# Two more key tiles per slot in three fp32r products, the pointwise residual on ScalarE and VectorE, and joined small operations, in a fused attention and convolution kernel

## The chip, the cores and the metric

The kernel runs on one core of one Trainium2 chip. The core has TensorE (matmuls; its weight loads are listed apart), VectorE (DVE in the profile), ScalarE (ACT), GpSimd (POOL) and SyncE (SP), each of which takes its own instructions in order, and 16 DMA engines. The metric is the device time of one execution in microseconds. A profile is one further execution with the hardware profiler on; its span runs from the first to the last instruction.

## The reference

The input is x of 4 pictures x 64 x 64 pixels x 256 channels, in float32. Layer 0 is full self-attention over the 4096 pixels of each picture:

```
q, k, v = x@Wq + bq, x@Wk + bk, x@Wv + bv        # 32, 32 and 256 wide
x = gamma * softmax(q k^T) v + x
```

Layer 1 takes that result h:

```
perceived = depthwise 3x3 convolution, 3 outputs per channel  # 768 channels
dx        = w_up2 @ gelu(w_up1 @ perceived + b_up1) + b_up2   # 768 -> 512 -> 256, per pixel
h_new     = h + dx                                            # the pointwise residual
h_attn    = softmax-weighted sum of the 9 neighbours' values  # 3x3 local attention, q, k, v from h_new
out       = h_new + h_attn
```

Neighbours outside the picture have score 0 and value 0, so they count in the local softmax's denominator alone. The program first computes without subtracting a maximum from the scores, watches for overflow in a few sums, and has a second, slower path that runs if any was seen.

## The kernel before, in words

**Slots.** A block is 8 picture rows, 512 pixels; there are 8 blocks per picture and 32 in all (`NSLOT`). Slot s runs the full attention of block s, and beside it layer 1 of earlier blocks: the 3x3 convolution of block s - 2, the hidden layer, pointwise residual, local scores and local values of block k = s - 3, and the local attention's result of block a = s - 5. The order of all instructions is written out by hand in the main loop (lines 1214 to 1359), which the engines' queues keep. A slot has 16 points. At each point the loop issues loads, ScalarE's high parts and TensorE's energy for later halves, one entry of `jobs` (layer 1), the product of this point's half, VectorE's sums and parts for the next half (`add_up`), and some steps of the convolution on VectorE. The list `share` (L1244) says how many of the 54 convolution steps (42 taps on 526 pixels, 12 combinations of half-size tiles) are issued at each point.

**Halves and tiles.** The 4096 keys of a picture are 16 halves n = 0 to 15 of 256 keys, and a half is two tiles (i = 0, 1) of 128 keys. For each half, TensorE makes scores for two tiles x 512 queries (`energy`, L414), ScalarE takes exp of them (L423), and `product` (L452) multiplies the weights p with the values v into the accumulators, two channel halves per tile. The product of half n stands at point n, its exp two halves earlier.

**Products in parts.** An f32 matmul appears in the profile as two records, an fp32r matmul as one. Where a tile is taken in parts, p is split into high (ScalarE), low and gap (two VectorE operations), and the f32 product of each channel half is replaced by three fp32r products with stored forms of v: high with v's high, low and gap with two further forms. The even halves 2 to 14 have both tiles in parts at once (`in_parts`, `high_part`, tiles ph, pl, pg; forms vf loaded from packed_f). The odd halves are treated tile by tile (`alone`, L228, `load_alone`, `high_alone`, `low_and_gap` at L440): the second tile of every odd half (tiles vo, oh, ol, og, four buffers under the tag vs), and also the first tile for those in `BOTH_IN_PARTS`, whose form, high, low and gap lie in the four quarters of a hidden-layer tile (tag hid, one buffer), free after the residual at point 7. This holds in full slots: slots 3 to 30 other than those whose number is 7 modulo 8, so 25 slots. `alone(s, n)` gives the tiles of half n that are taken alone. `load_alone` and `high_alone` for half n stand at point n - 1, `low_and_gap` in `add_up` at point n - 1, before that point's convolution steps. The forms were written by `project_v` (L342) one picture ahead.

**Sums.** For most halves the weights are summed by accumulating DMAs that GpSimd issues (`send`). VectorE sums halves 14 and 15 in the tile den, and in the first slot of a picture also halves 0 and 1. After half 15 `partial_sums` (L539) transposes and reduces the sums, and at point 0 of the next slot `finish` scales the accumulated result.

**The residual and after.** `update(s, c)` at points 6 and 7 multiplies the hidden layer with w_up2 for channel half c and adds bias and h, per column half, on VectorE (L863). `border_terms` (L988) then makes, with c = 1, weighted sums over the channels of the block's border pixels in the tile edge (ScalarE for one channel half, VectorE for the other); `border` at point 14 sums them over partitions by a matmul with a column of ones (L1004). `local_values` (L1016; points 0 and 10) projects 2 x 128 pixels and adds the bias in two VectorE operations. PSUM tiles for these jobs come from a rotation of two banks (`job_bank`).

Of the kernel before, what the change touches and what calls it, by code (L numbers as in the profile page):

```python
# [9 lines left out]
F32 = mybir.dt.float32  # L10
# [6 lines left out]
P = 128  # L17
# [33 lines left out]
BELOW = 1.0 - 2.0**-13  # L51
IN_PARTS = (2, 4, 6, 8, 10, 12, 14)
ONE_IN_PARTS = (1, 3, 5, 7, 9, 11, 13, 15)
BOTH_IN_PARTS = (11, 13)
BY_DMA = (3, 5, 7, 9, 11, 13)
BY_DMA_IF_FULL = tuple(range(14))

# [5 lines left out]
def attention_then_perception_kernel(  # L63
# [37 lines left out]
    def unshifted():  # L101
# [120 lines left out]
        def full(s):  # L222
            return in_two_sums(s) and s > 1 and s % NBLK < NBLK - 1
# [3 lines left out]

        def alone(s, n):  # L228

            return [i for i, ns in enumerate((BOTH_IN_PARTS, ONE_IN_PARTS)) if full(s) and n in ns]  # L230

        def load_parts(to, s, which):
            pair, r = divmod(s, 2)
# [74 lines left out]
        def load_values(s, G):  # L308
            values[s, G] = tile_of([P, TPB, C], "v", f"v_{s}_{G}", 2)
            to = values[s, G].rearrange("p t c -> p (t c)")  # L310
            at = block(s, G)
            if not in_two_sums(s):
                nc.sync.dma_start(out=to, in_=packed_v[:, bass.ts(at, TPB * C)])
            elif full(s):
                nc.sync.dma_start(out=to, in_=packed_h[:, at])
            else:
                nc.sync.dma_start(out=to[:, : 2 * C], in_=packed_h[:, at, : 2 * C])
                nc.sync.dma_start(out=to[:, 2 * C :], in_=packed_v[:, bass.ts(2 * at + 1, 2 * C)])
# [8 lines left out]
        def load_alone(s, n):  # L327
            for i in alone(s, n):
                if i:
                    f, *rest = [tile_of([P, NB], "vs", f"vo_{s}_{n}", 4)] + [None] * 3  # L330
                else:
                    four = tile_of([P, NHC, NB], "hid", f"vo_{s}_{n}_0")
                    f, *rest = (four[:, j] for j in range(NHC))
                forms[s, n, i], rests[s, n, i] = f, rest
# [96 lines left out]
        def high_alone(s, n):  # L431
            for i in alone(s, n):
                high = rests[s, n, i][0]
                if high is None:
                    high = tile_of([P, NB], "vs", f"oh_{s}_{n}", 4)
                p = weights[s, n // 2, n % 2][:, i, :]
                nc.scalar.activation(high.bitcast(F32R), p, AF.Identity, scale=BELOW)  # L437
                highs[s, n, i] = high

        def low_and_gap(s, n):  # L440
            for i in alone(s, n):
                high, (_, low, gap) = highs[s, n, i], rests.pop((s, n, i))
# [3 lines left out]
                nc.vector.tensor_tensor(low.bitcast(F32R), p, high, ALU.subtract)  # L446
                nc.vector.scalar_tensor_tensor(
                    gap.bitcast(F32R), low, -SPLIT, high, ALU.mult, ALU.add
                )
                lows[s, n, i], gaps[s, n, i] = low, gap  # L450

        def product(s, G, half):  # L452
            p = weights[s, G, half]
            n = 2 * G + half
            if n == 0:
                accs[s] = [bank("acc", f"acc_{s}_{c}") for c in range(2 * CH if in_two_sums(s) else CH)]
                started[s] = set()
            v = values[s, G][:, 2 * half : 2 * half + 2]
            todo = []
            if in_parts(s, G, half):  # L460
                f = forms.pop((s, G, half))
                for w, to, x in (
                    (v, 0, highs[s, G, half]), (f[:, :2], 0, lows[s, G, half]),
                    (f[:, 2:], CH, gaps[s, G, half]),
                ):
                    todo += [(w[:, i], to, x[:, i, :], F32R) for i in range(2)]
            else:
                apart = alone(s, n)
                todo += [(v[:, i], 0, p[:, i, :], F32) for i in range(2) if i not in apart]
                for i in apart:  # L470
                    at = s, n, i
                    f = forms.pop(at)
                    todo += [
                        (v[:, i], 0, highs[at], F32R), (f[:, :C], 0, lows[at], F32R),
                        (f[:, C:], CH, gaps[at], F32R),
                    ]
            ends = {0: n == 2 * NG - 1, CH: n == (2 * NG - 1 if full(s) else IN_PARTS[-1])}
            for k, (w, to, x, kind) in enumerate(todo):
                last = ends[to] and all(later[1] != to for later in todo[k + 1 :])
                for c in range(CH):  # L480
                    nc.tensor.matmul(  # L481
                        accs[s][to + c], lhsT=w[:, bass.ts(c, P)].bitcast(kind), rhs=x.bitcast(kind),
                        start=to not in started[s], stop=last,
                    )
                started[s].add(to)
# [53 lines left out]
        def partial_sums(s):  # L539


            a = shared(s)
            parts_[s] = tile_of([P, 2, NJ], "parts", f"parts_{s}")
            turneds[s] = tile_of([P, CH, NB], "xc", f"turned_{s}", 2)
            todo = [sums[s][:, 0, :]] + ([] if a is None else [lsums.pop(a)])
            for i, t in enumerate(todo):
                nc.vector.transpose(turneds[s][:, i, :], t)
                nc.vector.tensor_reduce(
                    parts_[s][:, i, :], squares(turneds[s][:, i, :]), axis=AX.X, op=ALU.add
                )  # L550
            watch(parts_[s][:, : len(todo), :].rearrange("p i j -> p (i j)"))

        def on_all(values, turned, out, copy=nc.vector.tensor_copy):

# [297 lines left out]
        def update(s, c):  # L852
            if c == 0:
                below(s)
            ps = job_bank(f"dx_{s}_{c}")
            for d in range(NHC):
                nc.tensor.matmul(  # L857
                    ps, lhsT=wup2[:, d, bass.ts(c, P)], rhs=hids[s][:, d, :],
                    start=(d == 0), stop=(d == NHC - 1),
                )  # L860
            for half in range(2):
                cols = slice(half * KW, (half + 1) * KW)
                nc.vector.scalar_tensor_tensor(  # L863
                    hs[s][:, c, half, HALO:, :],
                    ps.rearrange("p (h w) -> p h w", w=W)[:, :, cols],
                    bup2[:, c : c + 1],
                    xv[:, c, ring(s) : ring(s) + RB, 1 + cols.start : 1 + cols.stop],
                    ALU.add, ALU.add,
                )
            if c == CH - 1:  # L870
                border_terms(s)

# [93 lines left out]
        def edge_row(s):  # L966
            return {0: 0, NBLK - 1: RB - 1}.get(s % NBLK)

        edge = pool.tile([P, 2 * RB + W], F32, tag="edge", name="edge")

        def border_parts(s):

# [15 lines left out]
        def border_terms(s):  # L988


            for to, of in border_parts(s):
                nc.scalar.mul(edge[:, to], of(0), wc[:, 0:1])
                nc.vector.scalar_tensor_tensor(
                    edge[:, to], of(1), wc[:, 1:2], edge[:, to], ALU.mult, ALU.add
                )

        def border(s):

# [2 lines left out]
            row = edge_row(s)  # L1001
            n_side = 2 * RB
            n = border_parts(s)[-1][0].stop
            nc.tensor.matmul(ps[0:1, :n], lhsT=ones[:, 0:1], rhs=edge[:, :n], start=True, stop=True)  # L1004
# [11 lines left out]
        def local_values(s, t):  # L1016
            ps = job_bank(f"lv_{s}_{t}")
            for half in range(2):
                for kin in range(CH):
# [2 lines left out]
                        lhsT=keys_of(s, t, half, kin), rhs=wlv[:, kin, :],  # L1022
                        start=(kin == 0), stop=(kin == CH - 1),
                    )
            for half in range(2):
                if s < NSLOT - 2:
                    lvs[s, t, half] = tile_of([P, C], "lv", f"lv_{s}_{t}_{half}", 8)
                else:
                    if not half:
                        late[s, t] = late_tile(f"lv_{s}_{t}")  # L1030
                    lvs[s, t, half] = late[s, t][:, half * C : (half + 1) * C]
                lv = lvs[s, t, half]
                nc.vector.tensor_tensor(lv, ps[:, half * C : (half + 1) * C], blv, ALU.add)
                if s >= NSLOT - 1:

                    square = tile_of([P, 2, NB], "den", f"lv_{s}_{t}_{half}_2")[:, 0, :C]
                    nc.gpsimd.tensor_tensor(square, lv, lv, ALU.mult)
                    watch(square)

        def pieces(s):  # L1040

# [172 lines left out]
        for slot in range(NSLOT):  # L1214
# [611 lines left out]
```

## Time and profile before

| | |
|---|---|
| median of 3 runs | 3206.65 us (3204.02 to 3208.27) |
| profiled execution: time, span | 3203.15 us, 3201.4 us |
| granted TensorE clock | 0.998 |
| busy: TensorE, VectorE, ScalarE, GpSimd | 3179.4, 2903.6, 1550.8, 759.6 us |
| exp on ScalarE (L423) | 512 of 128x1024, 1025 ns each |
| convolution tap on VectorE (L687) | 1260 of 128x526, 759 ns each |
| low and gap of a single tile (ol, og) | 200 each, 709 and 732 ns |
| residual on VectorE (L863) | 128 of 128x256, 475 ns each |
| load of a single tile's forms (vo) | 250 of 256 KB, 3.9 us to landing |
| DMA queues | 683.26 MB, mean 213 GB/s |

In the profile a line such as "L447 DVE ... og<-ol,oh" is one group of instructions: source line, engine, tile written and tiles read. In a timeline the first two numbers are the start and the length in microseconds from the span's start. Consecutive instructions of a pipeline overlap by some 0.08 us on VectorE and more on TensorE, so the distance from start to start is what an instruction costs; in the chain of work that ended last, each piece has just that length. "x2" at the end merges two equal ones. A stretch sum gives the busy time of each engine between two times.

### The profile page before, as it was taken

How to read it: one execution, taken by the hardware profiler on the slowest of the kernel's cores; microseconds unless marked ns; L12 is line 12 of the kernel's file. 1: busy time of each engine (PE TensorE's matmuls, PEld its weight loads, DVE VectorE, ACT ScalarE, POOL GpSimd, SP SyncE). 2: the span in 40 equal slices, each digit the busy share in tenths (PEclk: the TensorE clock that was granted, in tenths of full speed). 3: DMA queues.
4: the chain of work that ended last, by engine and by line, in shares of the span. 5: the costliest groups of instructions: out<-in, count | busy, mean ns of one | idle time of the engine just before them, and what ended most of it. 6: DMA issues, size and time to landing. Idle time of an engine off the chain costs nothing.

```text
span 3201.4 us, 39239 instructions
## 1 busy us (share of the span) xinstructions
PE 3179.4 (99%) x12486; PEld 2261.7 (71%) x12486; DVE 2903.6 (91%) x4428; ACT 1550.8 (48%) x2068; POOL 759.6 (24%) x1055
## 2 busy tenths in 40 slices
PE   9999999999999999999999999999999999999998
PEld 5557777766777777776777777777677777777655
DVE  5778999998999999998999999998899999999894
ACT  4435555445545555544555545554555555455331
POOL 3201122212222221222122232211221222222121
PEclk9999999999999999999999999999999999999999
DMA  7768888777888888877878888886788888888100
GB/s 259 229 170 218 227 226 224 220 230 229 227 227 243 243 218 229 221 208 247 234 219 232 225 240 234 238 221 197 269 238 221 224 228 227 235 237 220 50 25 28
DMA packets 315588, 683.26 MB, mean 213 GB/s; under 512 B 100384, under 2 KB 101424, under 8 KB 315248
## 3 DMA queue, kind: packets, MB, share of 16 engines
q1 hardware_dynamic: 243008, 435.69, 42.6%
q0 software_dynamic: 64688, 231.54, 31.7%
q10 hardware_dynamic: 7680, 13.44, 1.1%
q8 instruction: 104, 1.70, 0.2%
q14 instruction: 108, 0.88, 0.1%
HBM read 412.46 MB, written 80.61 MB: 154 GB/s over the span
## 4 chain that ended last, share of the span: by engine, by line
PE 94%; DVE 3%; DMA 1%; issue 0%; POOL 0%; ACT 0%; SPq 0%; ACTq 0%; DVEq 0%; POOLq 0%
PE acc L481 46%; PE e L418 7%; PE dx L857 7%; PE hid_de L800 5%; PE hid_gf L800 5%; PE hid_bc L800 5%; PE lv L1020 3%; PE g L953 3%; PE lo L1154 3%; PE v L347 3%; PE s L1061 2%; PE hid_a L800 2%; DVE perc L687 1%; PE qk L272 1%; PE hid L832 1%; DMA vo<-packed_o 0%
## 5 line engine op out<-in xcount | busy, mean ns | idle before, releaser
L687 DVE SCALAR_TENSOR_TENSOR perc<-xp,wb,perc 128x526 f32<-128x526 f32 (+1 forms) x1356 | 937.7, 757 | 0.4
L423 ACT ACTIVATE p<-e 128x1024 f32<-128x1024 f32 x512 | 524.9, 1025 | 485.9 <-PE e L418 409.4
L481 PE MATMUL acc<-p,v 128*128 128x512 f32 x1472 | 678.9, 596 | 0.2 <-ACT v L363 0.2
L500 POOL DMA_DIRECT2D sent<-p x304 | 258.0, 855 | 1353.6 <-ACT p L423 823.0
L481 PEld LDWEIGHTS acc<-p,v 128*128 128x128 f32 x1472 | 275.1, 190 | 267.9 <-issue 257.6
L418 PE MATMUL e<-qa,ka 128*128 128x512 f32 x1024 | 357.1, 430 | 5.3 <-ACT p L423 1.5
L428 ACT ACTIVATE ph<-p 128x1024 fp32r<-128x1024 f32 x203 | 215.1, 1060 | 198.4 <-PE acc L481 134.7
L510 DVE TENSOR_TENSOR pl<-p,ph 128x1024 fp32r<-128x1024 f32 x203 | 256.1, 1262 | 16.8 <-ACT ph L428 16.8
L481 PE MATMUL acc<-ph,v 128*128 128x512 f32 x812 | 264.3, 447 | 0.2
L520 DVE SCALAR_TENSOR_TENSOR pg<-pl,ph 128x1024 fp32r<-128x1024 f32 x203 | 253.3, 1248 | 11.9 <-DVE pl L510 0.5
L418 PEld LDWEIGHTS e<-qa,ka 128*128 128x128 f32 x1024 | 190.9, 188 | 86.0 <-issue 39.9
L437 ACT ACTIVATE oh<-p 128x512 fp32r<-128x512 f32 x200 | 126.4, 632 | 248.4 <-PE acc L481 83.2
L857 PE MATMUL dx<-hid,wup 128*128 128x512 f32 x512 | 229.8, 592 | 0.0
L481 PE MATMUL acc<-pl,vf 128*128 128x512 f32 x812 | 223.3, 397 | 0.0
L481 PE MATMUL acc<-pg,vf 128*128 128x512 f32 x812 | 219.1, 391 | 2.0 <-DVE pg L520 2.0
L481 PEld LDWEIGHTS acc<-ph,v 128*128 128x128 f32 x812 | 148.2, 189 | 51.9 <-issue 26.8
L481 PE MATMUL acc<-oh,v 128*128 128x512 f32 x400 | 184.8, 543 | 0.0
L481 PEld LDWEIGHTS acc<-pg,vf 128*128 128x128 f32 x812 | 152.3, 188 | 39.1 <-DVE pg L520 3.3
L481 PEld LDWEIGHTS acc<-pl,vf 128*128 128x128 f32 x812 | 152.7, 188 | 37.1
L823 ACT ACTIVATE hid<-hid,bup 128x512 f32<-128x512 f32 x120 | 80.3, 716 | 199.1 <-DVE hid L807 199.1
L693 DVE TENSOR_TENSOR perc<-perc 128x262 f32<-128x262 f32 x360 | 170.8, 488 | 6.3
L857 PEld LDWEIGHTS dx<-hid,wup 128*128 128x128 f32 x512 | 96.7, 189 | 98.5 <-issue 93.4
(231 smaller groups left out, 5476.1 us busy)
## 6 DMA issues: line engine op xcount, KB each, us to landing
sent<-p POOLq DMA_DIRECT2D x356, 512.0 KB, 6.5
vf<-packed_f SPq DMA_DIRECT2D x203, 512.0 KB, 5.7
v<-packed_h SPq DMA_DIRECT2D x200, 512.0 KB, 4.7
ka<-packed SPq DMA_DIRECT2D x1016, 64.0 KB, 3.3
vo<-packed_o SPq DMA_DIRECT2D x250, 256.0 KB, 3.9
xp<-in_x SPq DMA_DIRECT2D x30, 528.0 KB, 6.9
packed_f<-vlg POOLq DMA_DIRECT2D x28, 512.0 KB, 4.3
xc<-in_x SPq DMA_DIRECT2D x56, 256.0 KB, 4.3
```

Source lines behind the costliest of these rows:

```text
L418: nc.tensor.matmul(e[:, i, :], lhsT=keys[s, G][:, bass.ts(2 * half + i, P)].bitcast(F32R), rhs=queries[s].bitcast(F32R), start=True, stop= ...
L423: nc.scalar.activation(p, e, AF.Exp)
L428: nc.scalar.activation(high.bitcast(F32R), weights[s, G, half], AF.Identity, scale=BELOW)
L437: nc.scalar.activation(high.bitcast(F32R), p, AF.Identity, scale=BELOW)
L481: nc.tensor.matmul(accs[s][to + c], lhsT=w[:, bass.ts(c, P)].bitcast(kind), rhs=x.bitcast(kind), start=to not in started[s], stop=last,)
L500: nc.gpsimd.dma_start(out=sent[s, even], in_=p, accum_op=ALU.add)
L510: nc.vector.tensor_tensor(low.bitcast(F32R), p, high, ALU.subtract)
L520: nc.vector.scalar_tensor_tensor(gap.bitcast(F32R), low, -SPLIT, high, ALU.mult, ALU.add)
L687: nc.vector.scalar_tensor_tensor(acc, win, wt, acc, ALU.mult, ALU.add)
L693: nc.vector.tensor_tensor(t[:, to, :], t[:, a, :], t[:, b, :], op)
L800: nc.tensor.matmul(ps[:, n * C : (n + 1) * C], lhsT=w(j), rhs=rows_of(mixes[s, j][:, kind, :]), start=(j == 0), stop=(j == MULT - 1),)
L857: nc.tensor.matmul(ps, lhsT=wup2[:, d, bass.ts(c, P)], rhs=hids[s][:, d, :], start=(d == 0), stop=(d == NHC - 1),)
```

## The change

1. `BOTH_IN_PARTS` becomes (3, 9, 11, 13). In full slots the first tile of half 9, and of half 3 except in slots 8, 16 and 24, is taken in parts too. Half 9 uses the hid tile as 11 and 13 do. Half 3 has its form and high part in the two halves of the tile den ("where sums stand") and its low and gap in the two tiles of tag o ("where results stand").
2. In slots 8, 16 and 24 the first tile of half 3 stays f32, so `load_values` overwrites that quarter of the value tile with the plain values by a second load.
3. The pointwise residual: ScalarE writes the matmul's result plus bias to SBUF, for all 512 pixels, and one VectorE addition adds h.
4. Both channel halves of the border products are written by ScalarE into a tile of twice the size, and `border` sums them with two accumulating matmuls.
5. The two reductions of `partial_sums` become one; the two bias additions of `local_values` become one, in one tile of both halves; in the last slot's blocks the two squares that are watched become one.
6. `share` moves convolution steps between points; the sum is the same.

```diff
-BOTH_IN_PARTS = (11, 13)
+BOTH_IN_PARTS = (3, 9, 11, 13)
...
         def alone(s, n):
-            return [i for i, ns in enumerate((BOTH_IN_PARTS, ONE_IN_PARTS)) if full(s) and n in ns]
+            if not full(s) or n not in ONE_IN_PARTS:
+                return []
+            return [0, 1] if n in BOTH_IN_PARTS and (n > NHC * 2 or s % NBLK) else [1]
...
             elif full(s):
                 nc.sync.dma_start(out=to, in_=packed_h[:, at])
+                n = 2 * G + 1
+                if n in BOTH_IN_PARTS and 0 not in alone(s, n):
+                    nc.sync.dma_start(
+                        out=to[:, 2 * C : 3 * C],
+                        in_=packed_v[:, (2 * at + 1) * 2 * C : (2 * at + 1) * 2 * C + C],
+                    )
...
-                else:
+                elif n > NHC * 2:
                     four = tile_of([P, NHC, NB], "hid", f"vo_{s}_{n}_0")
                     f, *rest = (four[:, j] for j in range(NHC))
+                else:
+                    two = tile_of([P, 2, NB], "den", f"vo_{s}_{n}_0")
+                    f, *rest = two[:, 0], two[:, 1], *(
+                        tile_of([P, NB], "o", f"o{x}_{s}_{n}_0", 2) for x in "lg"
+                    )
...
             for i, t in enumerate(todo):
                 nc.vector.transpose(turneds[s][:, i, :], t)
-                nc.vector.tensor_reduce(
-                    parts_[s][:, i, :], squares(turneds[s][:, i, :]), axis=AX.X, op=ALU.add
-                )
+            parts = parts_[s][:, : len(todo), :].rearrange("p i j -> p (i j)")
+            turned = turneds[s][:, : len(todo), :].rearrange("p i n -> p (i n)")
+            nc.vector.tensor_reduce(parts, squares(turned), axis=AX.X, op=ALU.add)
...
-            for half in range(2):
-                cols = slice(half * KW, (half + 1) * KW)
-                nc.vector.scalar_tensor_tensor(
-                    hs[s][:, c, half, HALO:, :],
-                    ps.rearrange("p (h w) -> p h w", w=W)[:, :, cols],
-                    bup2[:, c : c + 1],
-                    xv[:, c, ring(s) : ring(s) + RB, 1 + cols.start : 1 + cols.stop],
-                    ALU.add, ALU.add,
-                )
+            nc.scalar.activation(
+                pixels(s, c), by_rows(ps), AF.Identity, bias=bup2[:, c : c + 1]
+            )
+            nc.vector.tensor_tensor(
+                pixels(s, c), pixels(s, c),
+                xv[:, c, ring(s) : ring(s) + RB, 1 : 1 + W].rearrange("p h (a w) -> p h a w", a=2),
+                ALU.add,
+            )
...
             for to, of in border_parts(s):
-                nc.scalar.mul(edge[:, to], of(0), wc[:, 0:1])
-                nc.vector.scalar_tensor_tensor(
-                    edge[:, to], of(1), wc[:, 1:2], edge[:, to], ALU.mult, ALU.add
-                )
+                for c in range(CH):
+                    nc.scalar.mul(edge[:, c, to], of(c), wc[:, c : c + 1])
...
-            nc.tensor.matmul(ps[0:1, :n], lhsT=ones[:, 0:1], rhs=edge[:, :n], start=True, stop=True)
+            for c in range(CH):
+                nc.tensor.matmul(
+                    ps[0:1, :n], lhsT=ones[:, 0:1], rhs=edge[:, c, :n],
+                    start=(c == 0), stop=(c == CH - 1),
+                )
...
+            bias = blv.unsqueeze(1).to_broadcast([P, 2, C])
+            nc.vector.tensor_tensor(lv, ps.rearrange("p (a c) -> p a c", a=2), bias, ALU.add)
...
-            share = [2, 6, 8, 4, 7, 2, 7, 4, 6, 4, 3, 1, 0, 0, 0, 0]
+            share = [2, 6, 7, 5, 8, 3, 7, 4, 5, 3, 3, 1, 0, 0, 0, 0]
```

More of the change, by code (lines that the diff above doesn't have):

```diff
@@ L330, in load_alone @@
                     f, *rest = [tile_of([P, NB], "vs", f"vo_{s}_{n}", 4)] + [None] * 3
[L331 removed]
+                elif n > NHC * 2:
                     four = tile_of([P, NHC, NB], "hid", f"vo_{s}_{n}_0")
                     f, *rest = (four[:, j] for j in range(NHC))
[L334 removed]
+                else:
[3 more added lines that the diff above has]
+                    )
+                forms[s, n, i, P], rests[s, n, i] = f, rest
                 nc.sync.dma_start(
@@ L437, in high_alone @@
                 nc.scalar.activation(high.bitcast(F32R), p, AF.Identity, scale=BELOW)
-                highs[s, n, i] = high
+                highs[s, n, i, P] = high
         def low_and_gap(s, n):
             for i in alone(s, n):
-                high, (_, low, gap) = highs[s, n, i], rests.pop((s, n, i))
+                high, (_, low, gap) = highs[s, n, i, P], rests.pop((s, n, i))
                 if low is None:
@@ L449, in low_and_gap @@
                 )
-                lows[s, n, i], gaps[s, n, i] = low, gap
+                lows[s, n, i, P], gaps[s, n, i, P] = low, gap
         def product(s, G, half):
@@ L470, in product @@
                 for i in apart:
-                    at = s, n, i
+                    at = s, n, i, P
                     f = forms.pop(at)
@@ L547, in partial_sums @@
                 nc.vector.transpose(turneds[s][:, i, :], t)
-                nc.vector.tensor_reduce(
-                    parts_[s][:, i, :], squares(turneds[s][:, i, :]), axis=AX.X, op=ALU.add
-                )
-            watch(parts_[s][:, : len(todo), :].rearrange("p i j -> p (i j)"))
+            parts = parts_[s][:, : len(todo), :].rearrange("p i j -> p (i j)")
+            turned = turneds[s][:, : len(todo), :].rearrange("p i n -> p (i n)")
+            nc.vector.tensor_reduce(parts, squares(turned), axis=AX.X, op=ALU.add)
+            watch(parts)
         def on_all(values, turned, out, copy=nc.vector.tensor_copy):
@@ L967, in edge_row @@
             return {0: 0, NBLK - 1: RB - 1}.get(s % NBLK)
-        edge = pool.tile([P, 2 * RB + W], F32, tag="edge", name="edge")
+        edge = pool.tile([P, CH, 2 * RB + W], F32, tag="edge", name="edge")
         def border_parts(s):
@@ L1024, in local_values @@
                     )
+            if s < NSLOT - 2:
+                lv = tile_of([P, 2, C], "lv", f"lv_{s}_{t}", 4)
+            else:
+                lv = late_tile(f"lv_{s}_{t}").rearrange("p (a c) -> p a c", a=2)
             for half in range(2):
[L1026 to L1038, printed above, removed]
+                lvs[s, t, half] = lv[:, half]
+            bias = blv.unsqueeze(1).to_broadcast([P, 2, C])
+            nc.vector.tensor_tensor(lv, ps.rearrange("p (a c) -> p a c", a=2), bias, ALU.add)
+            if s >= NSLOT - 1:
+                square = tile_of([P, 2, NB], "den", f"lv_{s}_{t}_2")[:, 0, :]
+                nc.gpsimd.tensor_tensor(square.rearrange("p (a c) -> p a c", a=2), lv, lv, ALU.mult)
+                watch(square)
         def pieces(s):
```

## The prediction

> **What bounds the kernel now.** I read the page first (engine shares, chain), then the chain of one slot, then the stretch sums of that slot, then TensorE's and VectorE's timelines of its second half.
>
> ```profile
> PE 3179.4 (99%) x12486; PEld 2261.7 (71%) x12486; DVE 2903.6 (91%) x4428; ACT 1550.8 (48%) x2068; POOL 759.6 (24%) x1055
> ...
> PE 94%; DVE 3%; DMA 1%; issue 0%; POOL 0%; ACT 0%; SPq 0%; ACTq 0%; DVEq 0%; POOLq 0%
> ```
>
> TensorE sets the end: 94% of the chain. But 91% for VectorE is an average that includes the start and the tail. One slot (slot 14, 1302.73 to 1395.33; the slots around it also last 92.6) gives, as window, TensorE and VectorE busy:
>
> ```profile
> core 0: us, PE busy (x) PEld busy (x) DVE busy (x) ACT busy (x) POOL busy (x), PEclk, DMA share, GB/s
> 1302.73:1395.33 92.60, 92.60 (x378) 68.64 (x378) 88.80 (x133) 46.20 (x59) 21.13 (x25) 1.00 0.81 216
> ...
> 1368.08:1384.12 16.04, 16.04 (x77) 13.35 (x76) 15.62 (x22) 8.98 (x11) 8.85 (x10) 1.00 0.91 261
> ```
>
> VectorE fills 88.80 of 92.60, and 15.62 of 16.04 where halves 11 to 14 are prepared. So the question is by how much it is ahead of TensorE. Its timeline there, then TensorE's:
>
> ```profile
> 1368.74 0.68 DVE L446 TENSOR_TENSOR vo<-p,vo 128x512 fp32r<-128x512 f32 x1
> 1369.46 0.69 DVE L447 SCALAR_TENSOR_TENSOR vo<-vo 128x512 fp32r<-128x512 f32 x1
> 1370.07 0.69 DVE L446 TENSOR_TENSOR ol<-p,oh 128x512 fp32r<-128x512 f32 x1
> 1370.79 0.69 DVE L447 SCALAR_TENSOR_TENSOR og<-ol,oh 128x512 fp32r<-128x512 f32 x1
> 1371.40 2.00 DVE L693 TENSOR_TENSOR perc<-perc 128x262 f32<-128x262 f32 x3
> ...
> 1374.64 1.23 DVE L520 SCALAR_TENSOR_TENSOR pg<-pl,ph 128x1024 fp32r<-128x1024 f32 x1
> ...
> 1378.81 0.76 DVE L447 SCALAR_TENSOR_TENSOR og<-ol,oh 128x512 fp32r<-128x512 f32 x1
> ```
>
> ```profile
> 1373.63 0.61 PE L481 MATMUL acc<-og,vo 128*128 128x512 f32 x2
> ...
> 1377.75 1.07 PE L481 MATMUL acc<-pg,vf 128*128 128x512 f32 x4
> ...
> 1381.38 0.61 PE L481 MATMUL acc<-og,vo 128*128 128x512 f32 x2
> ```
>
> Lead of VectorE (its end to TensorE's use): half 11: 1373.63 - 1371.48 = 2.15; half 12: 1377.75 - 1375.87 = 1.88; half 13: 1381.38 - 1379.57 = 1.81. Read the same way, half 6 has 2.28, half 10 has 3.18, half 14 has 2.07, the others 3 to 9. The lead restarts in each slot: at its start VectorE waits 0.98 for TensorE's local values and then 0.21 and 0.16 (local product, half 4), and after that it never waits for TensorE until halves 11 to 14 are done. Slots whose map block lies on the picture's edge (10, 11, 18, 19, 26, 27) show that nothing absorbs a delay: they have two more 0.17 us border instructions at point 7, and from there on every lead is shorter by 0.32 to 0.33 (half 13: 1.49).
>
> [...] three combinations take 1.93 instead of 3 x 0.44 beside the mask product on GpSimd (1372.13, 0.99 us), and a gap of half 13 takes 1.34 instead of 0.69 beside the next one.
>
> **The change part by part.** Tiles gained: the 25 full slots take half 9, and 22 of them (all but 8, 16, 24) take half 3: 47 tiles.
>
> *TensorE.* From the chain of the slot, half 9 with one tile in parts, a half in parts behind the same kind of f32 work, and the border sum:
>
> ```profile
> 1356.66 2.79 PE acc L481 x12
> ...
> 1361.63 3.10 PE acc L481 x10
> ...
> 1382.45 0.13 PE c L1004 x2
> ```
>
> 3.10 - 2.79 = 0.31, and half 3 (3.10, against 2.78 for half 2) 0.32; I take 0.32: 47 x 0.32 = 15.0 saved. The border sum becomes two matmuls: again 0.13 for 24 borders, 0.23 (the 80-column one in the tail) for 8: 5.0 added. TensorE alone: -10.0.
>
> *VectorE, per full slot up to half 13.* Two tiles more, each low and gap: the four operations from 1368.74 to 1371.40 are 2.66. Residual: two instructions of 0.475, together 0.79 (1345.40 to 1346.19), become one 128x512 add of two SBUF operands; nearest row the sum at L1179, 0.60: -0.19, twice -0.37. It now waits for ScalarE, covered: the matmuls for c = 0 end at 1344.7, ScalarE needs 0.69, VectorE arrives at 1345.4 or later. Border products leave VectorE: -0.33. Joined local values: pair 0.66, one 0.61: -0.05 (that of point 0 is lost in the wait). The 0.16 wait is absorbed. The joined reduction (about -0.1) comes after half 15. The new shares have the same sum (50) by point 9. Sum: 2.66 - 0.37 - 0.33 - 0.05 - 0.16 = +1.75. The shares hold half 6 (2.28 - 1.85 - 0.32 = +0.1) and half 10 (3.18 - 2.47 - 0.64 = +0.1) just on time.
>
> *The stall.* TensorE comes to halves 11 to 14 earlier by 2 x 0.32 = 0.64. Lead left: half 11: 2.15 - 2.39 = -0.24; half 12: -0.51; half 13: -0.58; half 14: -0.32. The latest one counts: TensorE waits about 0.58 and the slot changes by -0.64 + 0.13 + 0.58 = +0.07. The first mask product of GpSimd (0.6) then falls on half 11 instead of the combinations, up to 0.85 of wait: +0.34. I take +0.2; 14 ordinary full slots: +2.8.
>
> *Edge slots (six).* VectorE regains 0.66 instead of 0.33, but starts at a lead of 1.49: wait 0.57. ScalarE is worse: its border products now wait for VectorE's residual of c = 1 (about 1354.3), and behind them stand two first taps (1.5), two high parts (1.27) and the exp (1.03). Ordinary: three products (0.75) put that exp's end at about 1358.95, TensorE's next energy needs its bank at 1359.46 - 0.32 = 1359.14. In edge slots seven products come first: about 0.85 late. I take a wait of 0.8: -0.64 + 0.23 + 0.8 = +0.4, six times: +2.4.
>
> *Slots 8, 16, 24* sum two halves on VectorE and have leads of 0.05, 0.22, 0.05 at half 14. VectorE +0.58, TensorE -0.32: waits 0.85, 0.68, 0.85, with the border +1.8 in all. *Slots 3 and 4:* smallest leads 0.05 and 0.31, by the same sum +3.2; part of that shortness may be a load (a 7.75 us landing lies on the chain at 314.58), half: +1.6. *Other seven borders:* +1.0. *Tail:* the last residual before the last guide is ScalarE 0.69 + VectorE 0.69 instead of 0.89: +0.5, less 0.1 in the VectorE stretch before it: +0.4.
>
> *Loads and buffers.* 47 loads more of 256 KB (3.9 median) on SP, 0.32 of issue each. Half 3 uses the sums' tile and two result tiles; their last readers are VectorE's at 1306, the load is issued near 1314. Half 11's first tile must now wait for half 9's last product: issue near 1364 instead of 1360.65, use near 1371: 7 us for 3.9. In slots 8, 16, 24 a second load into the same value tile waits on SP for the first (4.7 + 4.2), used 16 us later. ScalarE's 2 x 0.63 + 2 x 0.69 per slot lie in its 46 idle us, but for the exp above. Values of blocks 1 and 4 in full size: +0.7 of VectorE, 8 times, in slots with slack. I count these at nothing; the cover lost, a late load costs its lateness.
>
> Sum: 2.8 + 2.4 + 1.8 + 1.6 + 1.0 + 0.4 = +10.0 on the profiled 3203.15 (span 3201.4): 3213.2. The median of the runs shown is 3.5 above the profiled execution: 3216.7.
>
> **Rivals.** *B, TensorE stays the bound (faster):* the whole -10.0 and the tail's +0.4 show: 3197. For it: 99% busy, waits for VectorE only 2.0 us in the whole run. Against: the leads above. It decides if VectorE's net addition is under 1.81 - 0.64 = 1.2 instead of 1.75. *C, break-even:* the mask product falls elsewhere and the early slots were short for loads: +0.07 per ordinary slot and less at slots 3, 4 and 8: about 3209. *D, the hid tile:* landings reach 9.8; where half 11's first tile takes over 7, TensorE waits up to 2.4 more; one slot in ten gives +5 to +6 on the forecast: 3222.
>
> **How the numbers follow.** Forecast 0.55 (0.10 of it under the bound of slower, 0.45 over), B 0.27, C 0.13, D 0.05. This measurement tells 0.2% from no change: 3200.2 and 3213.1. Faster 0.27, same 0.13 + 0.10 = 0.23, slower 0.50. The forecast's own range is 3209 to 3226 (0 to 0.35 more or less per slot); with B and D: 3194 to 3228.
>
> **What would show it.** Full slots of 92.6 to 93.0 instead of 92.1; TensorE idle some 15 to 20 us in all before the low and gap products of halves 11 to 14 (now 2.0), VectorE at 98% or more of a full slot; in edge slots an energy waiting for the exp at point 9. Wrong: full slots near 92.1 with no such waits, that is VectorE's added 1.75 smaller or regained in a wait that I took for fixed.

## The result, and the profile after

The changed kernel takes 3235.85 us (median of 6 runs, 3233.35 to 3239.11); the kernel before took 3204.78 (6 runs) beside it. The ratio is 1.010, 95% interval 1.0089 to 1.0111: 1% slower. The forecast was 3216.7 with a range to 3228. The direction was right and the size was not: of the +31 us it had foreseen +10.

First the page of the changed kernel: engine shares, DMA packets and bytes, the chain by engine, and the loads of single tiles and of keys (KB each, median us from issue to landing). A q after an engine's name means its sequencer, which issues and waits; "issue" is time in which an engine waited for nothing that the profile shows.

```profile
PE 3194.9 (99%) x12644; PEld 2269.2 (70%) x12644; DVE 2937.2 (91%) x4286; ACT 1627.1 (50%) x2259; POOL 750.3 (23%) x1052
...
DMA packets 323304, 698.11 MB, mean 216 GB/s; under 512 B 101184, under 2 KB 102608, under 8 KB 322960
...
PE 69%; DVE 19%; DMA 6%; issue 3%; ACT 2%; SPq 1%; DVEq 0%; ACTq 0%
...
vo<-packed_o SPq DMA_DIRECT2D x297, 256.0 KB, 5.7
ka<-packed SPq DMA_DIRECT2D x1016, 64.0 KB, 3.7
```

The busy shares look unchanged. The chain does not: VectorE had 3% of it and has 19%, DMA had 1% and has 6%. The bytes rose by 2%, the time for a `vo` to land from 3.9 to 5.7 us. (TensorE's busy time rose by 15 us although it has less to do: the ends of its matmuls are modelled, and part of its waits stands in them. The four low and gap products of half 11's first tile take 1.38 us in slot 14, 1.07 before.)

Slot 14 as a window sum, the same slot as in the prediction, then the stretch in which halves 11 to 14 are prepared:

```profile
core 0: us, PE busy (x) PEld busy (x) DVE busy (x) ACT busy (x) POOL busy (x), PEclk, DMA share, GB/s
1316.25:1409.80 93.55, 93.16 (x380) 68.34 (x380) 90.50 (x129) 48.49 (x65) 20.14 (x25) 1.00 0.85 223
1381.60:1398.40 16.80, 16.41 (x73) 11.96 (x72) 16.42 (x22) 9.00 (x11) 8.95 (x10) 1.00 0.94 267
```

And in that stretch VectorE's timeline, GpSimd's and TensorE's (start, length, engine, line, instruction; low and gap of the first tile are named `vo` there, after the tile in whose quarters they lie):

```profile
1383.62 0.68 DVE L1048 TENSOR_TENSOR lv<-lv,blv 128x512 f32<-128x512 f32 x1
1384.22 0.68 DVE L461 TENSOR_TENSOR vo<-p,vo 128x512 fp32r<-128x512 f32 x1
1384.94 0.69 DVE L462 SCALAR_TENSOR_TENSOR vo<-vo 128x512 fp32r<-128x512 f32 x1
1385.55 1.45 DVE L461 TENSOR_TENSOR ol<-p,oh 128x512 fp32r<-128x512 f32 x1
1387.03 0.69 DVE L462 SCALAR_TENSOR_TENSOR og<-ol,oh 128x512 fp32r<-128x512 f32 x1
1387.64 1.24 DVE L708 TENSOR_TENSOR perc<-perc 128x262 f32<-128x262 f32 x3
```

```profile
1385.35 1.10 POOL L1101 TENSOR_TENSOR lp<-lp,near 128x396 f32<-128x396 f32 x1 [4.90 <-ACT lp L1096]
```

```profile
1386.25 0.62 PE L496 MATMUL acc<-oh,v 128*128 128x512 f32 x2
1387.05 0.73 PE L496 MATMUL acc<-ol,vo 128*128 128x512 f32 x2 [0.17 <-DVE ol L461]
1387.78 0.74 PE L496 MATMUL acc<-og,vo 128*128 128x512 f32 x2
1388.36 0.63 PE L433 MATMUL e<-qa,ka 128*128 128x512 f32 x2
```

VectorE's `og` of half 11 ends at 1387.72 and TensorE's product of it starts at 1387.78: the lead, 2.15 us before, is zero. TensorE starts both products 0.05 to 0.06 after VectorE has written their tiles. Two things add up. VectorE comes to half 11 late (counted from the energy of the slot's point 0, 1.86 us later; 1.75 foreseen). And GpSimd's mask product, which before lay beside the three combinations (2.00 us, now 1.24), lies beside `ol`, which takes 1.45 instead of 0.68.

I compared the distance from energy to energy, point by point, in all 31 slots. In an ordinary slot (12) the differences are: point 3 -0.34 and point 9 -0.33, the two gains; points 6 and 10 +0.12 and +0.15, where halves 6 and 10 now come late; point 11 +1.05; points 13 and 14 +0.13 and +0.06. Together +0.84. By groups: 14 ordinary slots from 5 on +15.6, the six edge slots +13.2, slots 3 and 4 +2.3, slots 8, 16 and 24 +1.6, the slots numbered 7 modulo 8 -0.2.

The edge slots, and slots such as 6, 14 and 22, show a second loss. Slot 11, SP's timeline, TensorE's, and a piece of the chain:

```profile
1087.22 4.99 SPq L240 DMA_DIRECT2D qa<-packed  x4
1092.31 0.37 SPq L332 DMA_DIRECT2D vf<-packed_f  x1
1094.15 1.06 SPq L350 DMA_DIRECT2D vo<-packed_o  x2
1095.27 2.99 SPq L240 DMA_DIRECT2D ka<-packed  x4
```

```profile
1105.46 0.61 PE L496 MATMUL acc<-og,vo 128*128 128x512 f32 x2
1107.60 0.70 PE L433 MATMUL e<-qa,ka 128*128 128x512 f32 x2 [1.52 <-DMA ka<-packed]
```

```profile
1096.81 10.54 DMA ka<-packed
```

TensorE is ready for the next energy at 1106 and waits for keys that needed 10.54 us to land. The prediction had counted every load at nothing.

### The profile page after: what moved, and what is told of

It reads as the page before. It is cut to its first block, busy times and chain, and to the rows that moved or that the text cites. A ratio compares the mean times of both kernels' runs of the same rounds, so it can differ in the third digit from the quotient of the medians.

```text
span 3233.4 us, 39835 instructions
## 1 busy us (share of the span) xinstructions
PE 3194.9 (99%) x12644; PEld 2269.2 (70%) x12644; DVE 2937.2 (91%) x4286; ACT 1627.1 (50%) x2259; POOL 750.3 (23%) x1052
## 2 busy tenths in 40 slices
DMA packets 323304, 698.11 MB, mean 216 GB/s; under 512 B 101184, under 2 KB 102608, under 8 KB 322960
## 4 chain that ended last, share of the span: by engine, by line
PE 69%; DVE 19%; DMA 6%; issue 3%; ACT 2%; SPq 1%; DVEq 0%; ACTq 0%
PE acc L496 32%; DVE perc L702 7%; PE e L433 5%; PE hid_bc L815 5%; PE dx L872 5%; PE hid_gf L815 4%; PE hid_de L815 4%; DMA vo<-packed_o 3%; PE v L362 3%; PE lv L1036 2%; PE hid_a L815 2%; PE lo L1169 2%; DVE pg L535 2%; DVE ol L461 2%; PE g L967 2%
## 5 line engine op out<-in xcount | busy, mean ns | idle before, releaser
L496 PE MATMUL acc<-p,v 128*128 128x512 f32 x1284 | 588.9, 595 | 0.2 <-ACT v L378 0.2
L496 PEld LDWEIGHTS acc<-p,v 128*128 128x128 f32 x1284 | 238.9, 190 | 230.8 <-issue 221.5
L535 DVE SCALAR_TENSOR_TENSOR pg<-pl,ph 128x1024 fp32r<-128x1024 f32 x203 | 254.4, 1253 | 13.2
L496 PEld LDWEIGHTS acc<-pg,vf 128*128 128x128 f32 x812 | 149.3, 188 | 47.4 <-DVE pg L535 15.6
L708 DVE TENSOR_TENSOR perc<-perc 128x262 f32<-128x262 f32 x360 | 161.2, 468 | 7.3
L496 PE MATMUL acc<-oh,v 128*128 128x512 f32 x400 | 166.1, 496 | 0.0
```

The costliest lines, as they stand in the source:

```text
L496: nc.tensor.matmul(accs[s][to + c], lhsT=w[:, bass.ts(c, P)].bitcast(kind), rhs=x.bitcast(kind), start=to not in started[s], stop=last,)
L535: nc.vector.scalar_tensor_tensor(gap.bitcast(F32R), low, -SPLIT, high, ALU.mult, ALU.add)
L708: nc.vector.tensor_tensor(t[:, to, :], t[:, a, :], t[:, b, :], op)
```

## The experiments

Three theories stood at the start. V: VectorE's lead is used up, as forecast. L: loads come late, because more of them move or because SP's queue stands behind the shared hid tile. S: ScalarE's border products hold back an exp. Each run has the kernel before on the same chip beside it; the ratios are to that.

### Which part of the change, which resource

`a1_parts_only` has the added tiles with the rest as before; `a2_rest_only` has all but the added tiles:

```diff
-BOTH_IN_PARTS = (3, 9, 11, 13)
+BOTH_IN_PARTS = (11, 13)
```

> The kernel before with the added tiles alone: both tiles of halves 3 and 9 in parts, with their loads and buffers; residual, border, reductions, local values and shares as before. Theory V (VectorE's lead at halves 11 to 14 is used up): VectorE's work up to half 13 grows by 2.66 - 0.16 = 2.5 us per full slot instead of 1.87, so this is slower than the changed kernel would be without its second border matmul: 3235 - 5 + 25 x 0.5 = about 3240. Theory L (loads come late, because more of them stand behind one hidden-layer buffer on SP): the same loads as the changed kernel, without the border matmuls: about 3230. Theory S (ScalarE's border products wait for VectorE and hold back the exp): these are as before, so edge slots lose no more than the others.

> The changed kernel without the added tiles (halves 11 and 13 alone in both tiles), all else of the change kept. V: VectorE is relieved by 0.8 us per slot, TensorE pays 5.0 for the borders and 0.4 in the tail: before + 5, about 3210. L: the same, about 3210. S: the border products on ScalarE cost 0.8 in each of the 7 edge slots on top: about 3216.

a1: 3236.0, ratio 1.0097 (1.0080 to 1.0114). a2: 3205.15, ratio 1.0004 (0.9995 to 1.0013). The added tiles make the whole loss. The rest, which the prediction charged with +5.0 for its border matmuls, costs nothing that can be told: point 14 grows by 0.05 in ordinary slots, not 0.13 (by 0.16 in edge slots). Edge slots lose 1.5 in a1 and 2.2 in the changed kernel, which leaves ScalarE's border products (S) a part of the difference at most.

`a3_no_added_vector` drops VectorE's low and gap of the added tiles, `a4_no_added_loads` drops their loads, `b1_neither` drops both:

```diff
+                if i == 0 and n in (3, 9):
+                    lows[s, n, i, P], gaps[s, n, i, P] = high, high
+                    continue
                 p = weights[s, n // 2, n % 2][:, i, :]
```

```diff
                 forms[s, n, i, P], rests[s, n, i] = f, rest
+                if i == 0 and n in (3, 9):
+                    continue
+                if n in (3, 9):
+                    forms[s, n, 0, P] = f
                 nc.sync.dma_start(
```

> The changed kernel without the low and gap operations of the added tiles on VectorE: TensorE reads the high part three times in their place, so the output is not the reference's in these tiles; matmuls, loads, buffers and ScalarE's work stay. V: the stalls at halves 6 and 10 to 14 go, and TensorE's own saving shows: before - 15 + 5 + 0.4, about 3195. L: the late loads stay, 3220 or more. S: edge slots keep about 0.3 each at point 8, 3197.

> The changed kernel without the 47 added loads: the added first tiles take the form of the half's second tile, so the output is not the reference's; all else stays, and SP waits for the hidden-layer tile at halves 11 and 13 only. V: VectorE's work is the same, 25 to 30 us of the loss stay: about 3230. L: the loss goes, 3205 or less.

> The changed kernel with neither the low and gap operations of the added tiles on VectorE nor their loads (high read three times, the second tile's form used; not the reference's output in these tiles). V and L together: alone they took 19 and 7 us off; a slot that still waits for one cannot show what the other costs, so both together should leave TensorE's own path: before - 15 + 1, about 3191, full slots shorter by about 0.6. If a third cause holds TensorE (ScalarE's border products, the joined operations): 3200 or more, with 0.3 in each edge slot at point 8.

a3: 3216.92, ratio 1.0043 (1.0026 to 1.0060). a4: 3229.10, ratio 1.0079 (1.0061 to 1.0097). b1: 3205.32, ratio 1.0003 (0.9994 to 1.0012). Neither V nor L alone explains the loss, and taking both away does not give the 15 us of TensorE's gain. In a4 the ordinary slots keep their +0.83, so those are V's. In b1, undisturbed full slots (4, 6, 13, 30) are 0.63 to 0.68 shorter than before, as TensorE's account wants. But others wait at points 11 to 13 for `ka` or `vo`, up to 2.3 us, although this kernel loads only three pieces of 128 KB more than the kernel before (685.76 MB moved in all, against 683.26). So there was a third thing.

`b2_half3` adds half 3 alone (`BOTH_IN_PARTS = (3, 11, 13)`):

> The changed kernel with half 3 but without half 9 in both tiles (22 tiles added instead of 47). V: VectorE's work up to half 13 changes by 1.33 - 0.16 - 0.75 = +0.4 and TensorE comes 0.32 earlier; half 13's lead falls from 1.81 to 1.1, so no stall, and 22 x 0.33 = 7.3 are gained: about 3198. L: half 9 no longer stands in the hidden-layer tile ahead of half 11, no late loads, the same 3198. S: 0.3 in each of 7 edge slots on top: 3200. If the stall comes with each added tile alike: half of the loss, about 3220.

3212.86, ratio 1.0025 (1.0015 to 1.0035). Its slots without a wait are 0.1 to 0.2 shorter; single slots lose up to 2.2 at points 11 to 14, again to loads. Half 3's own load was long done by then.

`b3_no_mask` leaves out GpSimd's mask product, to see what its contention with VectorE is worth:

> The changed kernel without GpSimd's product of the local weights with the window mask (left out in all but the last slots, so the local attention is not the reference's). V [...]: half 11's last operations on VectorE lose the 0.6 to 0.8 us that they have beside that product; the stall at half 11 falls from 1.05 to about 0.3, that at half 13 stays about 0.2: 0.5 per full slot, about 3222. V without it (the bare count of VectorE's work): no change, 3235. L: no change, 3235.

3247.74, ratio 1.0142 (1.0125 to 1.0159), slower still. In ordinary slots the loss at point 11 fell from +1.05 to +0.47 and point 12 rose from 0 to +0.61. GpSimd went straight on to its sums, which then stood beside VectorE's next halves. The contention decides where the wait appears; leaving this instruction out did not lessen it. The run's profiled execution was its fastest (3238.65). In it the full slots lose no more than in the changed kernel (31.3 against 32.8 in all), and slot 0 is 4.4 longer. What its other executions, up to 3252.02, lost besides stays open.

### Is it SP's queue behind the shared tile?

Halves 9, 11 and 13 share hid, so their loads wait for each other on SP and the key loads behind them wait too: in slot 14 of the changed kernel SP waits 1.9 us for half 9's product before half 11's two loads leave; before, they followed the form load at once. `b4_half9_den` and the four c kernels move one of them to den and o, for instance:

```diff
-                elif n > NHC * 2:
+                elif n > NHC * 2 and (n != 11 or s % NBLK == 0):
                     four = tile_of([P, NHC, NB], "hid", f"vo_{s}_{n}_0")
```

> The changed kernel with half 9's first tile in the sums' tile and two result tiles, as half 3's, instead of in the hidden-layer tile (22 slots; 8, 16 and 24 as before). L by the queue: half 11's load no longer waits for half 9's product, so the key load behind it on SP is early again and the 7 us that the loads cost go: about 3228. L by traffic: the same bytes, so no change, 3235. V: no change.

> The changed kernel with one line different: in the slots whose number is not a multiple of 8 the extra tile of half 11 stands in den and o, as half 3's does, instead of hid. In the changed kernel the halves 9, 11 and 13 all use hid, so SP, which issues loads in order, waits at half 11 for half 9's product and at half 13 for half 11's, and the four key loads behind each wait too. Here no hid load waits for the half just before it. V (VectorE's work stands between the halves 9 to 13): the ordinary slots stay 0.8 longer than before, only the edge slots lose part of their late loads: 3226 to 3232. Q (the queue behind hid carries most): 3210 to 3216. Traffic (the loads land late whatever their order): 3234 to 3236.

> The same move of half 11's extra tile to den and o in the kernel without the added low and gap and without the added loads (3205.3; it leaves the same work out). There the full slots without a wait were 0.63 shorter than before, but at points 11 to 13 TensorE waited for ka and vo in most. In slot 12 SP could issue half 11's tile only at 1178.53, 3.4 later than before, and the keys behind it landed 0.33 too late. Q (that queue is the third cause): the full slots come to -0.5 to -0.65, in all 3190 to 3196. Traffic: 3203 to 3206.

> The same move in the kernel with half 3 alone added (3212.9). Nothing is left out. There half 3's 0.33 is gained, 0.12 lost at half 6, and TensorE waits for ka and vo at points 11 to 13 in single slots. In this kernel half 9 has no extra tile, so the halves 11 and 13 no longer share one buffer at all. Q: the single waits go, 3199 to 3204. Traffic: as without the move, 3211 to 3214.

> The kernel before with half 11's extra tile in den and o instead of hid: what the move does by itself. In the kernel before TensorE waits for these loads 0.2 to 2 us in all, so there is little to gain: 3203 to 3206 under each theory. A loss would mean that the move itself costs something (den or o come free late at the slot's start).

b4: 3234.01, ratio 1.0092 (1.0075 to 1.0108). c1: 3237.0, 1.0101 (1.0084 to 1.0118). c2: 3203.18, 0.9994 (0.9985 to 1.0003). c3: 3211.52, 1.0025 (1.0018 to 1.0032). c4: 3202.02, 0.9995 (0.9986 to 1.0004). The moves did what they should on SP: in c2 the median start of the first key load of point 10 went from 0.40 after that point's energy (b1) to 0.32 before it. The time did not follow, as far as intervals of some 3 to 5 us can tell. As the cause of the loss this theory falls.

What c2 shows in its place is in slot 19, a piece of its chain:

```profile
1879.08 1.87 PE acc L503 x8
1880.94 0.02 SPq L354
1880.96 0.03 issue
1881.00 8.54 DMA vo<-packed_o
1889.54 0.14 issue
1889.67 1.17 PE acc L503 x4
```

The load leaves on time and lands after 8.54 us. And this is slot 19 of the kernel before, as sums from energy to energy of points 9 to 12. DMA share and GB/s are the last two numbers; the share is the packets' time over that of 16 engines, so that overlapping packets bring it over 1:

```profile
1862.88:1868.15 5.27, 5.27 (x18) 3.02 (x16) 5.16 (x8) 2.49 (x4) 0.84 (x1) 1.00 1.02 267
1868.15:1873.13 4.98, 4.98 (x24) 4.14 (x22) 4.98 (x8) 2.46 (x3) 0.85 (x1) 1.00 1.03 258
1873.13:1877.66 4.53, 4.53 (x23) 3.97 (x22) 4.43 (x8) 2.41 (x4) 1.84 (x4) 1.00 1.02 288
1877.66:1882.24 4.58, 4.58 (x23) 3.98 (x22) 4.44 (x6) 2.97 (x4) 2.11 (x5) 1.00 1.04 293
```

By their share, 1.02 to 1.04, the DMA engines are full there before anything is changed. The rate is 258 to 293 GB/s at these shares, and 344 at a share of 1.07 in the changed kernel (point 12 of slot 19), so the share tells more here than the rate.

### Are the DMA engines themselves the limit?

Theory D says so: whatever TensorE gains it spends waiting for loads that cannot land sooner. Four runs take traffic out of points 7 to 11 and leave all vector and matrix work in place:

```diff
         def load_forms(s, G, half):
+            if full(s) and 2 * G + half > 8:
+                forms[s, G, half] = kept[s]
+                return
             forms[s, G, half] = tile_of([P, TPB, C], "vf", f"vf_{s}_{G}_{half}", 2)
+            kept[s] = forms[s, G, half]
```

> The kernel with neither the added vector operations nor the added loads and half 11's extra tile in den and o (3203.2), and besides without the loads of the form tiles vf of halves 10, 12 and 14 in full slots: half 8's tile is read in their place, so that these loads, 768 KB a slot in points 7 to 11, are left out; all vector and matrix operations stay. D (the DMA engines are full in points 5 to 12, share 1.00 to 1.04 in slot 19 of the kernel before, so a shorter TensorE only runs into its loads): the waits for ka, vo and v at points 11 to 13 go, full slots -0.6, 3186 to 3192. Not D: 3201 to 3205.

> The changed kernel without the same form loads (halves 10, 12 and 14 read half 8's tile). VectorE's work is that of the changed kernel. V and D together: the ordinary slots, which wait for VectorE alone, stay 0.7 to 0.9 longer than before, the edge slots and the slots with late loads lose 0.5 to 2 each: 3222 to 3228. D alone: below 3205. Not D: 3234 to 3237.

> The kernel before without the same form loads: the control. TensorE waits there for loads 2 to 4 us in all, so under D and under its rival it stays at 3199 to 3204; a gain over 6 would mean that the loads cost the kernel before more than its waits show.

> The kernel without the added vector operations but with the added loads (3216.9; half 3's and half 9's high parts are read three times), and besides without the form loads of halves 10, 12 and 14. It moves 256 KB a slot less than the kernel before (two loads added, three left out). D: its late ka and vo go, full slots -0.6, 3187 to 3195. If hid's queue on SP holds the loads back: 3203 or more.

These texts count a `vf` tile at 256 KB. It has 512 KB, so 1.5 MB a slot are left out (75 loads; 698.11 MB become 658.78 in d2), and d4 moves 1 MB a slot less than the kernel before. Of slot 19's points 5 to 12, points 7 and 8 have a DMA share under 1.00 (0.93 and 0.76).

| | loads as in the changed kernel | fewer form loads |
|---|---|---|
| added tiles with their vector work | 3235.85, 1.0100 (1.0089 to 1.0111) | d2: 3224.19, 1.0063 (1.0046 to 1.0079) |
| added tiles without it | a3: 3216.92, 1.0043 (1.0026 to 1.0060) | d4: 3187.69, 0.9954 (0.9937 to 0.9970) |

The control d3 is 3202.79, ratio 0.9997 (0.9988 to 1.0006): the kernel before has nothing to gain from less traffic. d1 is 3189.90, ratio 0.9958 (0.9944 to 0.9972), where c2, the same kernel with all loads, had 0.9994. The column on the right is D's answer: with room on the DMA engines TensorE's gain is there, -15.1 from d3 to d4, and every full slot of d4 from 9 to 14 is 0.59 to 0.67 shorter than before. d2 keeps +0.80 to +0.88 in most ordinary slots and +0.65 to +0.77 in edge slots. Two groups of TensorE in d2, waits at the end of the line:

```profile
L439 PE MATMUL e<-qa,ka 128*128 128x512 f32 x1024 | 357.6, 430 | 4.5 <-DMA ka<-st 2.2 <-ACT p L444 1.8
L502 PE MATMUL acc<-og,vo 128*128 128x512 f32 x444 | 142.8, 403 | 2.8 <-DVE og L468 2.8
```

and in the changed kernel:

```profile
L433 PE MATMUL e<-qa,ka 128*128 128x512 f32 x1024 | 359.6, 432 | 9.8 <-DMA ka<-packed 5.4 <-ACT p L438 2.4 <-DMA ka<-st 1.1
L496 PE MATMUL acc<-og,vo 128*128 128x512 f32 x444 | 141.2, 399 | 2.0 <-DVE og L462 1.6 <-DMA ka<-packed 0.3
```

The waits for `ka<-packed` are gone with the traffic, the waits for VectorE are not. The reading by traffic rather than by SP's queue rests on loads that leave SP no earlier and land sooner (medians of slots 9 to 14, 17 to 22 and 25 to 30). Half 13's second tile leaves SP 0.68 before the energy of point 12 in c2 and in d1, and takes 7.3 us to land in c2 and 3.1 in d1. In d2 the first key load of point 10 leaves SP even later than in the changed kernel, 0.37 after that point's energy against 0.12 before it; yet the four key loads have landed 3.4 before the energy of point 12, against 0.4. The loads left out are all of SP's own DMA queue. Whether as many bytes fewer from GpSimd's accumulating DMAs would do the same was not tried.

### Can the loads be placed better?

The queries of the next slot, four loads of 64 KB, need not be issued in the full stretch:

```diff
-                    if G == NG // 2 and slot + 1 < NSLOT:
+                    if G == (1 if slot and g < NBLK - 1 else NG // 2) and slot + 1 < NSLOT:
                         spread_queries(slot + 1)
```

`e2_after_queries` is the changed kernel with that alone. `e1_half3_queries` is c3 with it, and with `share` beginning 3, 6, 7, 5, 7 instead of 2, 6, 7, 5, 8.

> A version meant to be faster than both, with nothing left out: the kernel with half 3 alone added and half 11's extra tile in den and o (3211.5), with the queries of the next slot (four loads of 64 KB on SP) issued at point 2 instead of point 8 in all slots but those numbered 7 mod 8 and slot 0, and one step of the perceiving convolution moved from point 4 to point 0, where VectorE stands idle 2 us or more. Under D, 256 KB fewer in the full stretch of points 5 to 12 takes away the late ka and vo, and the step earlier takes away the 0.12 at half 6: full slots -0.3, 3196 to 3201. If 256 KB is too little: 3204 to 3211.

> The changed kernel with the queries of the next slot issued at point 2 instead of point 8, nothing else. D: the same shift as leaving loads out, but smaller (256 KB moved against 1.5 MB left out; the tiles vf are 512 KB each, not 256 as the texts of the four runs before said): the edge slots' late ka and vo become fewer, 3227 to 3233. V is not touched, so it doesn't come below 3224. If order and place of the loads don't matter: 3234 to 3237.

e2: 3225.78, ratio 1.0065 (1.0049 to 1.0081), some 10 of the 11.7 us that leaving out the form loads had given, with nothing left out, and more than its own expectation. In the changed kernel these loads take 4.99 us of SP in slot 11 (shown above) as well as 256 KB of the stretch; which of the two counts for this move the runs don't separate. A share near 1.00 is also no proof that a load comes late. At points 10 to 12 it is still 1.05 to 1.06 in e2, as in the changed kernel (medians of ordinary slots), and the kernel before has 1.04 to 1.05 there and hardly waits for a load; only point 9 fell, from 1.00 to 0.86.

e1: 3205.22, ratio 1.0002 (0.9994 to 1.0011), 6 better than c3 and no faster than before. The late loads at points 11 to 13 are gone in nearly all slots. In their place the energy at point 5 waits, 0.23 to 0.59 in most full slots and 1.5 in slots 3 and 4. e2 and c3 show no such wait, so it is the moved convolution step. ScalarE in slot 12 of e1:

```profile
1145.75 1.34 ACT L838 ACTIVATE hid<-hid,bup 128x512 f32<-128x512 f32 x2 [4.79 <-DVE hid L822]
1146.99 1.53 ACT L698 ACTIVATE perc<-xp,wb 128x526 f32<-128x526 f32 x2
1148.42 0.62 ACT L452 ACTIVATE oh<-p 128x512 fp32r<-128x512 f32 x1
1149.06 1.28 ACT L438 ACT_TABLE_LOAD   x1
1150.35 1.03 ACT L438 ACTIVATE p<-e 128x1024 f32<-128x1024 f32 x1
```

The steps of the convolution come from one sequence. One step more at point 0 moves all later ones up, and with them two first taps on ScalarE, 1.53 us, which now stand ahead of the exp that this energy's bank waits for; without the move (b2, c3) they came after it. c3's tiles with the earlier queries and the old share were not run, so no version here is shown to beat the kernel before.

## Why the prediction was partly right and mostly too small

The differences between runs that follow are good to some 6 or 7 us by their intervals. In the forecast's own terms, TensorE's -10.0 was -15.1, and its +20.0 of waits were +48.2: 36.5 for VectorE and 11.7 for the loads.

**TensorE: the tiles right, the border wrong.** 47 tiles at 0.32 is -15.0; d3 to d4 measures -15.1 with the rest of the change in it. The +5.0 for the border matmuls appeared in part at most: I had added a second matmul's full piece of the chain, and the point grew by 0.05, in edge slots by 0.11 (d4); over the 32 borders that would be some +2 (an estimate).

**Ordinary slots: mechanism right, size off.** The forecast said that VectorE's lead at halves 11 to 14 is used up, and the timeline shows just that. The step that failed is its sum, +0.2 a slot against +0.83. Its waits were 0.58 and half of a contention, in all about 0.7; measured are 0.12 and 0.15 at halves 6 and 10, 1.05 at half 11 and about 0.13 at half 13, 1.5 in all. Three terms were mis-sized. VectorE's delay at half 11 was 1.86, not 1.75, and by half 13's `og` 2.4. Halves 6 and 10, which I left with a lead of +0.1 "just on time", were late: a remainder of 0.1 from a sum with errors of 0.1 to 0.2 is no lead. And the mask product delays half 11 by 0.77, where I let it add 0.27 to a slot at most (+0.07 to +0.34) and took half of that; b3 adds that GpSimd's next work takes its place if it goes. From d4 to d2, VectorE's added work costs 36.5 us, 1.46 in each of 25 full slots.

**Loads: the step that failed outright.** "I count these at nothing" was wrong, by 11.7 us from d2 to the changed kernel, and by 29 from d4 to a3, where no wait for VectorE hides it. Of these 29 some 12 are the added loads (b1 to a3); the other 18 (d4 to b1) are mostly loads that were there before and that a faster TensorE runs into. From d1 to c2, which differ in the form loads alone, it is 13. The window sum that I showed had a DMA share of 0.91 for the stretch, and the forecast drew nothing from it; point by point the share is 1.02 to 1.04 at points 9 to 12 of slot 19, and 0.97 to 1.06 in slot 14. The 3.9 us for a `vo` was a median of loads that differ: for half 11, 6.6 to 6.9 even in the kernel before. Rival D had the right symptom, a wait of up to 2.4 for a late tile, but put it on the hid tile, where b4 and c1 to c3 show no clear gain, and gave it one slot in ten.

**Rival B**, TensorE as the bound at 3197, named its condition as VectorE's net work alone. a3 and b1 take that work away and stay at 3216.92 and 3205.32: the condition was incomplete, DMA room was the other half. d4 meets both and has 3187.69. **Rival C**, break-even, did not hold: the mask product fell on half 11, not elsewhere, and slots 3 and 4 were not short for loads (below).

**Edge slots.** The forecast's 0.8 for ScalarE's border products is +0.3 at point 8 and +0.1 at point 9, and VectorE is then waited for less (in d2, point 10 nothing instead of 0.15, point 11 0.7 instead of 1.05). In d2 the edge slots are no worse than ordinary ones (+0.72); the rest of their +2.2 in the changed kernel is late loads.

**Slots 8, 16, 24**: +1.8 forecast, +1.6 measured, in part by luck. The forecast put all three waits at half 14. In d2, where loads don't disturb (+2.1), only slot 16 loses there (+1.04). Slots 8 and 24 lose 0.1 there and 0.7 each at half 11, where none was foreseen. Their "leads of 0.05" at half 14 were no leads: the kernel before already waits there, 0.58 and 0.65, and TensorE starts 0.05 after VectorE's write when it has waited. This is slot 8 of the kernel before:

```profile
828.35 1.21 PE L481 MATMUL acc<-pg,vf 128*128 128x512 f32 x4 [0.58 <-DVE pg L520]
```

**Slots 3 and 4**: +1.6 forecast, +2.3, and the same +2.3 in d2, so the half taken off for a load was wrong. **Tail**: +0.4 forecast, -0.9; b2, the same in its last slot, has +0.6, so this is within what executions differ by.

The waits do not add: VectorE's alone cost 36.5 with room on the DMA engines and 19 without. Here a TensorE held back by VectorE gave the loads time: they cost 11.7 beside VectorE's waits and 29 without. So d3's 3202.8, -15.1 for TensorE, +36.5 for VectorE and +11.7 for the loads come to 3235.9. That sum closes by construction, each step being the difference of two runs, and another order of the last two would share them otherwise.

## What to carry to other kernels

When the bound engine is 99% busy, look at what the others have left in each stretch, the DMA engines' share point by point included. Where it stood near 1.00 here, loads that the slower TensorE hid (d3 gains nothing without them) came late for the faster one (c2 against d1). The leads that the sum left at 0.1 us turned out as waits of 0.12 to 0.15. Before adding loads to a full stretch, move out of it those that are needed later, and look at everything that a moved step takes along on other engines.

## What the runs showed of the hardware

- A load's time to land differed with what moved beside it. The median for a 256 KB `vo` was 3.9 us before (683.26 MB in all), 5.7 in the changed kernel (698.11 MB) and 3.5 in d1 (646.40 MB). The bytes in all don't fix it: a2 moves 683.25 MB and has 4.4, c2 685.76 MB and has 5.3. It differs more within a slot: in the changed kernel 2.6 to 2.7 for half 5 and half 15, 7.4 to 7.7 for half 11 (medians of the 18 slots named above).
- Issuing took longer too: from the start of the first to the end of the fourth key load of point 10 SP needed 2.7 us before, 4.2 in the changed kernel and 3.0 in d1 (from medians of the same 18 slots).
- A VectorE operation on two SBUF tiles (`ol`, 128x512), 0.68 alone, took 1.45 beside a GpSimd product of 1.10. VectorE lost 0.77 of the 0.90 us in which the two overlap, and three combinations lost 0.76 beside the same product of 0.99 in the kernel before.
